# Moving two residual adds, a group of decay rates and one weight load around the start of a selective scan

## The chip, the cores and the metric

The kernel runs on one core of a Trainium2 chip. The metric is the device time of one launch, in microseconds (us); lower is better. The core has five engines that run their own instruction streams in order and meet through semaphores: PE (matmuls), DVE (vector), ACT (scalar functions), POOL (a second vector engine) and SP, which in this kernel only issues transfers.

## The reference, cut to what matters

Four sequences of 256 tokens with 512 features (1024 tokens, eight blocks of 128) go through two layers.

```python
xn = layernorm(x)
x = x + latent_attention(xn) + W_down(silu(W_gate xn) * (W_up xn))   # layer 0
xn = layernorm(x)
x = x + mamba(xn) + (base + top-2 LoRA experts)(xn)                  # layer 1
```

The Mamba part of layer 1 sets the second half of the kernel. For each of 1024 inner channels d and 16 states n:

```python
xc = silu(causal_conv4(xn @ in_proj_x))           # [channel, token]
dt_r, B, C = rmsnorm of the three parts of xc @ x_proj
dt = softplus(dt_r @ dt_proj + dt_bias)
h[t] = exp(dt[t] * A) * h[t-1] + dt[t] * B[t] * xc[t]     # A = -exp(A_log)
y[t] = sum_n h[t] * C[t];  out = ((y + D * xc) * silu(z)) @ out_proj
```

## The kernel before

**Layer 0.** The program works through two halves of 512 tokens. Gate, up and attention of a half are interleaved; then `down` (L432) makes the feed-forward and attention output of one block of 128 tokens. It is a generator: two matmuls with the attention result, then 14 chunks of two matmuls (high and low half of the hidden values), then one DVE addition of the PSUM result `po` to `x` (L446). With the yields there are 16 steps for each block of the second half: 1, 14 and the addition. `ff` is the stream of these steps for blocks 4 to 7, and `go(ff, n)` takes the next n. The steps fill PE while layer 1 begins, sequence 0 first, which needs only blocks 0 and 1.

**Opening of layer 1 (L1004 to L1094).** For sequence 0: four pairs of channel chunks are projected (`px_mm`), convolved (`conv_in`, `conv_taps`) and put through SiLU. `aneg` = -exp(A_log) is made by four ACT instructions from `al`, which sixteen small transfers bring in (L596); they stand ahead of the convolution of the last pair (L1023). Then the projection `pp`, its norm, and the step sizes: `step_in` makes two chunks of dt (one PSUM tile, two matmuls, then Abs and Relu of each chunk), `step_exp` the four ACT instructions of the softplus. Chunk 0 of dt and dt*x is spread over the partitions by matmuls (`pdts`, `pdus`), all later chunks through DRAM (`send`, `spread`). `decays(0)` and `decays(1)` make the decay factors of the first two units.

**The loop (L1222).** A unit u is one group of four states of one chunk of 128 channels: 4 units to a chunk, 8 chunks to a sequence, 128 units in all. Each unit has four decay instructions on ACT (`decays`, emitted up to two units ahead), a product `bx` and a scan `h` on DVE (`scan_in` L863, `scan` L871), a product with C on POOL (`hc`, L885), and four matmuls that sum the states into `ysum` (`states_sum`, one unit later). Two units after a chunk's last one, `close_chunk` multiplies its `ysum` by the gate silu(z). Everything else hangs on a table by unit: `put` places a call ahead of the unit's scan, `put_late` behind it. In the first three units the loop also takes `ff` steps at the head of a unit: 12, 12, and the rest. So the addition of block 6 comes in unit 1 and that of block 7 in unit 2, both ahead of that unit's `bx` and scan.

**Buffers and queues that the change touches.** PSUM pool `psmm` has three tiles, used in turn by nearly all matmul results (`po`, `pdt`, `pz`, ...). SBUF tag `w_in` has three tiles for projection weights of 512 KB; in the first units they are also lent out (`lent`, L840): to the decays of units 1 and 3, the scan results of units 0 and 2, and hc of unit 0. Unit 1's scan result is lent the buffer of `u`, a tile of the step computation, and its `hc` that of `lw`. `open_act`, called in unit 2, gives layer 0's memory to a new pool `act` and has SP issue four layer-1 weights into it: `rl`, `bw`, `lb`, `ow` (272, 1024, 256 and 2048 KB). Two further decay tiles, used from unit 4 on, are in this pool too; so their first writes wait until PE has read layer 0's data for the last time. `load_z` issues the gate's weights of a pair of chunks, `pz_mm` multiplies by them, `gate_silu` makes the gate (with a table load on each side). SP's order in units 2 to 4 is: dt and dt*x of the second pair out to DRAM, gate weights of pair 0, the spread of dt of chunk 2, the four layer-1 weights, gate weights of pair 1.

Of the kernel before, what the change touches and what calls it, by code (L numbers as in the profile page):

```python
# [11 lines left out]
AF = mybir.ActivationFunctionType  # L12
ALU = mybir.AluOpType
# [15 lines left out]
NG = 4  # L29
# [12 lines left out]
def block_kernel(  # L42
# [389 lines left out]
    def down(th, i):  # L432

        tb = 4 * th + i
        po = psmm.tile([P, D], F32, tag="mm", name="po")
        for hf in range(2):
            mm(po, lhsT=o8ns[th][:, hf, i * P : (i + 1) * P], rhs=m_att[:, hf, :],
               start=(hf == 0), stop=False)
        yield
        for m in range(MC):  # L440
            for j in range(2):
                mm(po, lhsT=hids[th][j][:, m, i * P : (i + 1) * P], rhs=wd[:, m, :],  # L442
                   start=False, stop=(m == MC - 1 and j == 1))
            if m < MC - 1 or th:
                yield
        nc.vector.tensor_tensor(x[:, tb, :], x[:, tb, :], po, ALU.add)  # L446
        yield

    def go(gen, n=1000):
        for _ in range(n):  # L450
# [311 lines left out]
        nc.scalar.copy(crows[b][:, 2 * i : 2 * i + 2, :], pc)  # L762


    def step_in(b, h, q):
        if q == 0:
            dts[b, h] = odd(h).tile([P, HALF, S], F32, tag="dt", name="dt")
            live["u"] = w1.tile([P, HALF, S], F32, tag="u", name="u")
        pd = psmm.tile([P, 2, S], F32, tag="mm", name="pdt")
        for i in range(2):  # L770
            c = h * HALF + 2 * q + i
            mm(pd[:, i, :], lhsT=dtw[:, c * P : (c + 1) * P], rhs=nrms[b][0:RK, :],
               start=True, stop=True)
        for i in range(2):
            j = 2 * q + i
            db = vec[:, h * HALF + j, V_DB : V_DB + 1]
            nc.scalar.activation(live["u"][:, j, :], pd[:, i, :], AF.Abs, bias=db)
            nc.scalar.activation(dts[b, h][:, j, :], pd[:, i, :], AF.Relu, bias=db)
# [232 lines left out]
    for p in range(NP):  # L1011
# [5 lines left out]
        if p < 3:  # L1017
            conv_in(0, p)
            conv_taps(0, p)
            go(ff, 1)  # L1020
    for n in range(NG):
        w = slice(n * NB, (n + 1) * NB)
        nc.scalar.activation(  # L1023
            aneg[w], al[w].rearrange("p k c (g n) -> p c k g n", n=NG)[:, :, :, :, n], AF.Exp
        )
    nc.gpsimd.tensor_scalar(aneg, aneg, -1.0, 1.0, ALU.mult, ALU.mult)

    px = live["px", 0, 3]
    nc.scalar.copy(pads[1][:, :, KC - 1 :], px)
# [4 lines left out]
    for i in range(2):  # L1034
# [11 lines left out]
        sel[:, 0 : NG * P].rearrange("p (k n j) -> p k n j", k=NG, n=NG),  # L1046
        ident.rearrange("p (k j) -> p k j", k=NG).unsqueeze(2).to_broadcast([P, NG, NG, NB]),
    )
    go(ff, 8)
    pp_mm(0, 0)  # L1050
    pp_mm(0, 1)
    pp_square(0)
    pp_norm(0)
    go(ff, 4)

    step_in(0, 0, 0)
    for j in range(2):
        step_exp(0, 0, slice(j, j + 1))
    b_rows(0, 0)
    c_rows(0, 0)  # L1060
# [3 lines left out]
    for j, eng in ((0, nc.vector), (1, nc.gpsimd)):  # L1064
# [1 line left out]
        eng.tensor_tensor(e[:, j, :], e[:, j, :], lw[:, j, :], ALU.add)  # L1066
        eng.tensor_tensor(dt[:, j, :], dt[:, j, :], e[:, j, :], ALU.add)
        eng.tensor_tensor(du[:, j, :], dt[:, j, :], xcs[0][:, j, :], ALU.mult)
    go(ff, 8)

    pdts = psx.tile([P, NG, S], F32, tag="bx", name="pdts")
    for k in range(NG):
# [16 lines left out]
    spread("du", 0, 1)  # L1089
    b_rows(0, 1)  # L1090
    c_rows(0, 1)
    step_in(0, 0, 1)
    step_exp(0, 0, slice(2, 4))
    decays(1)  # L1094

    def open_act():
        nonlocal act
# [19 lines left out]
    for b in range(B):  # L1117
        nxt = b + 1
        if b:
            put(b, 0, b_rows, b, 1)  # L1120
            put(b, 0, spread, "du", b, 1)

            for c in range(DC):
                put(b, c // 2, out_mm, b - 1, 1, c)
            put(b, 3, out_x, b - 1, 1)
            put(b, 4, dense, b - 1, 0, 0)
            put(b, 5, dense, b - 1, 0, 1)
            put(b, 5, expert_out, b - 1, 0)
            for c in range(DC):
                put(b, 6 + c, out_mm, b - 1, 0, c)  # L1130
            put(b, 15, out_x, b - 1, 0)
        else:
            for k in range(3):
                put(b, k, step_out, b, 0, 1, k)
            put(b, 2, step_x, b, 1)
            put(b, 2, load_z, b, 0)
            put(b, 4, load_z, b, 1)
            for p, u in ((0, 2), (1, 6)):
                for i in range(2):
                    put(b, u, pz_mm, b, p, i)  # L1140
            put(b, 4, gate_silu, b, 0)
            put(b, 8, gate_silu, b, 1)
        if b:
            put(b, 0, gate_silu, b, 0, 1)

# [76 lines left out]
    total = B * PER  # L1222
    late = []
    for u in range(total + 2):
        if u < 3:
            go(ff, 12 if u < 2 else 100)
        if 3 <= u < total - 2:
            decays(u + 2)
        for f, a in at.get(u, ()):
            f(*a)  # L1230
        if u < total:
            if u:
                scan_in(u)
        last = u - 2
        if last >= 0 and last % NU == NU - 1:
            c = last % PER // NU
            close_chunk(last // PER, c)
            if last // PER == B - 1:
                late.append(c)
        if u < total:  # L1240
            scan(u, 1 if u < total - 1 else 4)
            if u == 2:
                open_act()
            if u < 3:
                decays(u + 2)
        for f, a in late_at.get(u, ()):
            f(*a)
        if late and u >= total - PER + 22:
            c = late.pop(0)
            for i in range(2):  # L1250
                out_mm(B - 1, i, c)
        if 1 <= u <= total:
            states_sum(u - 1)
# [105 lines left out]
```

## Time and profile before

| quantity | value |
|---|---|
| median of 3 runs | 905.43 us (904.97 to 905.67) |
| the profiled execution's own time | 906.83 us |
| its span, first to last instruction | 905.0 us |
| busy, share of the span: PE, DVE, ACT, POOL | 84%, 76%, 58%, 54% |
| unit 0's scan begins | 363.23 us |
| the scans of units 1, 2, 3, 4, 5 begin | 374.47, 385.35, 389.01, 392.70, 398.57 us |
| mean of a scan, of a `bx`, of an `hc`, of a decay | 2234, 1231, 2308, 499 ns |

Times within the profile count from the span's start. The profiled execution lies 1.83 us around its span and 1.40 us over the median; a change is read as a difference of spans. In the profile's lines the parts are the start, the duration, the engine, the source line and operation, output and input, the count, and in brackets how long the engine was idle ahead of it and what ended that. SPq is SP's queue of transfers.

### The profile page before, as it was taken

The page shows a single profiled execution, that of the slowest core. Times are in us where ns is not written, and L with a number is a line of the kernel's source. Part 1 is how long each engine was busy: PE and PEld are TensorE (multiplying, and loading weights), DVE is VectorE, ACT ScalarE, POOL GpSimd, SP SyncE. Part 2 cuts the span into 40 slices and gives each one's busy share as a digit, 9 for nine tenths or more (in the row PEclk, how much of TensorE's full clock was granted, in tenths as well). Part 3 has the DMA queues.
Part 4 walks back from the last instruction along what each step waited for, and adds up shares of the span by engine and source line. Part 5 has one row for each costly group of instructions (what it writes and reads, how often), then busy time and mean ns, then how long its engine had stood idle before and what let it go on. Part 6 is the DMA issues. An engine that isn't in the chain of part 4 may idle for free.

```text
span 905.0 us, 10447 instructions
## 1 busy us (share of the span) xinstructions
PE 755.9 (84%) x3554; PEld 433.7 (48%) x3554; DVE 686.4 (76%) x675; ACT 525.5 (58%) x1005; POOL 489.4 (54%) x374
## 2 busy tenths in 40 slices
PE   5999989999989998876885898787898777976875
PEld 3665545666556576653542434443444443422421
DVE  4685553476573424486998999999999999999996
ACT  4234455213527356468768497778687785765661
POOL 4232222002223341456965969868789749797664
PEclk9999999999999999978786999987999888898997
DMA  6232232001222240394513453632635322436310
GB/s 209 67 85 80 83 93 70 12 0 35 59 58 70 59 114 26 78 306 116 151 47 93 124 144 100 168 94 61 172 116 176 82 79 85 117 89 170 88 28 23
DMA packets 67343, 86.67 MB, mean 96 GB/s; under 512 B 12077, under 2 KB 52025, under 8 KB 66906
## 3 DMA queue, kind: packets, MB, share of 16 engines
q1 hardware_dynamic: 57930, 67.12, 26.2%
q0 software_dynamic: 9072, 18.35, 7.3%
q8 instruction: 28, 0.46, 0.2%
q10 hardware_dynamic: 288, 0.52, 0.2%
q14 instruction: 25, 0.20, 0.1%
HBM read 66.58 MB, written 10.22 MB: 85 GB/s over the span
## 4 chain that ended last, share of the span: by engine, by line
PE 40%; DVE 32%; ACT 13%; POOL 6%; issue 5%; DMA 2%; SPq 1%; DVEq 0%; ACTq 0%; POOLq 0%
DVE h L881 19%; DVE bx L866 6%; ACT decay L860 5%; PE po L442 5%; PE pu L417 4%; PE pg L417 4%; PE sc L329 4%; POOL hc L885 3%; PE av L371 3%; PE scT L361 3%; PE pz L829 2%; PE pp L733 2%; PE ysum L897 2%; PE po L989 1%; ACT pe L363 1%
## 5 line engine op out<-in xcount | busy, mean ns | idle before, releaser
L885 POOL TENSOR_TENSOR hc<-h,cr 128x1024 f32<-128x1024 f32 (+1 forms) x131 | 302.0, 2308 | 121.0 <-DVE h L881 106.8
L881 DVE TENSOR_TENSOR_SCAN h<-decay,bx 128x1024 f32<-128x1024 f32 (+1 forms) x129 | 288.0, 2234 | 11.7
L860 ACT ACTIVATE decay<-dts,aneg 128x255 f32<-128x255 f32 x504 | 213.9, 499 | 117.8 <-DVE h L881 114.8
L897 PE MATMUL ysum<-hc,stack 128*32 128x256 f32 x1024 | 92.2, 431 | 89.5 <-POOL hc L885 89.2
L866 DVE TENSOR_TENSOR bx<-brow,dus 128x1024 f32<-128x1024 f32 x128 | 157.6, 1231 | 3.7
L429 POOL TENSOR_TENSOR hlo<-g,hhi 128x512 fp32r<-128x512 f32 x28 | 36.1, 1290 | 150.0 <-ACT hhi L428 150.0
L331 DVE TENSOR_REDUCE mpl<-sc 128x4 f32<-128x1024 f32 x64 | 77.3, 1223 | 23.7 <-PE sc L329 23.4
L897 PEld LDWEIGHTS ysum<-hc,stack 128*32 128x32 f32 x1024 | 21.9, 113 | 149.0 <-POOL hc L885 129.2
L400 POOL DMA_DIRECT2D wgu<-in_wgu x56 | 31.2, 557 | 90.8 <-PE pg L417 80.1
L363 ACT ACTIVATE pe<-scT 128x1024 f32<-128x1024 f32 x64 | 62.8, 1023 | 30.1 <-PE scT L361 29.8
L829 PE MATMUL pz<-xn1T,w_in 128*128 128x256 f32 x256 | 72.3, 433 | 6.8 <-DMA w_in<-in_inz 6.8
L989 PE MATMUL po<-ow,xc 128*128 128x512 f32 x128 | 72.3, 675 | 2.7 <-DVE xc L901 2.7
L689 PE MATMUL px<-xn1T,w_in 128*128 128x256 f32 x256 | 64.6, 400 | 2.3 <-ACT xn1T L681 1.6
L829 PEld LDWEIGHTS pz<-xn1T,w_in 128*128 128x128 f32 x256 | 52.1, 213 | 28.4 <-issue 12.2
L689 PEld LDWEIGHTS px<-xn1T,w_in 128*128 128x128 f32 x256 | 50.7, 202 | 22.4 <-issue 11.2
L425 DVE SCALAR_TENSOR_TENSOR g<-g,pg 128x512 f32<-128x512 f32 x28 | 19.2, 685 | 52.0 <-ACT g L424 52.0
L428 ACT CAST hhi<-g 128x512 fp32r<-128x512 f32 x28 | 17.4, 620 | 63.1 <-DVE g L427 62.7
L417 PE MATMUL pg<-xhi,wgu 128*128 128x512 f32 x112 | 46.6, 416 | 7.0 <-issue 4.5
L417 PE MATMUL pu<-xhi,wgu 128*128 128x512 f32 x112 | 47.7, 426 | 2.2 <-DMA wgu<-in_wgu 0.9
L442 PE MATMUL po<-wd,hhi 128*128 128x512 f32 x112 | 48.6, 434 | 0.0
L329 PE MATMUL sc<-km,qg 128*128 128x512 f32 x128 | 43.9, 424 | 3.3 <-ACT pe L363 2.8
L417 PE MATMUL pg<-xlo,wgu 128*128 128x512 f32 x112 | 44.8, 400 | 0.0
(213 smaller groups left out, 1249.4 us busy)
## 6 DMA issues: line engine op xcount, KB each, us to landing
dts<-dtd SPq DMA_DIRECT2D x124, 128.0 KB, 2.9
dus<-dud SPq DMA_DIRECT2D x124, 128.0 KB, 3.0
wgu<-in_wgu POOLq DMA_DIRECT2D x56, 256.0 KB, 2.8
w_in<-in_inz SPq DMA_DIRECT2D x16, 512.0 KB, 4.4
w_in<-in_inx SPq DMA_DIRECT2D x15, 512.0 KB, 4.4
dtd<-dt SPq DMA_DIRECT2D x15, 256.0 KB, 2.2
dud<-du SPq DMA_DIRECT2D x15, 256.0 KB, 2.2
wd<-in_wd POOLq DMA_DIRECT2D x7, 512.0 KB, 3.6
```

The source lines that it names most:

```text
L329: mm(sc[:, hp, :], lhsT=qs[b][:, gq, hf, qb * P : (qb + 1) * P], rhs=kms[b][:, 2 * hp : 2 * hp + 2, :], start=True, stop=True)
L331: nc.vector.tensor_reduce(mpl2[b % 2][:, qb, :, 16 + 2 * gq + hf].rearrange("p (a i) -> p a i", a=2), sc.rearrange("p a (i k) -> p a i k", ...
L417: mm(ps, lhsT=wgus[i][:, hc, :], rhs=xs[j][:, hc, :], start=(hc == 0 and j == 0), stop=(hc == HC - 1 and j == 1))
L442: mm(po, lhsT=hids[th][j][:, m, i * P : (i + 1) * P], rhs=wd[:, m, :], start=False, stop=(m == MC - 1 and j == 1))
L689: mm(px[:, i, :], lhsT=w[:, i, hc, :], rhs=xns[b][:, hc, :], start=(hc == 0), stop=(hc == HC - 1))
L829: mm(pz[:, i, :], lhsT=w[:, i, hc, :], rhs=xns[b][:, hc, :], start=(hc == 0), stop=(hc == HC - 1))
L860: nc.scalar.activation(da[:, k, 1:], live["dts", b, c][:, k, 1:], AF.Exp, scale=aneg[:, c, k, g : g + 1])
L866: nc.vector.tensor_tensor(bx, brow[g // 2][:, g % 2, :].unsqueeze(1).to_broadcast([P, NG, S]), live["dus", b, c], ALU.mult)
L881: nc.vector.tensor_tensor_scan(h[:, n].rearrange("p n t -> p (n t)"), da[:, n].rearrange("p n t -> p (n t)"), bx[:, n].rearrange("p n t -> ...
L885: nc.gpsimd.tensor_tensor(hc[:, n], h[:, n], crows[b][:, g, :].unsqueeze(1).to_broadcast([P, NG // parts, S]), ALU.mult,)
L897: mm(ysum[k * NB : (k + 1) * NB, :], lhsT=stack, rhs=hc[:, k, :], start=False, stop=(g == NU - 1))
L989: mm(live["po", b, i], lhsT=xcs[b][:, c, i * P : (i + 1) * P], rhs=late_w["ow"][:, c, :], start=False, stop=(c == DC - 1))
```

## The change

1. **The last two additions.** `down` no longer adds blocks 6 and 7; it leaves `po` in `live`, and `add_last` adds it behind the scan of unit 2 (block 6) and of unit 3 (block 7). The remaining `ff` steps of unit 2 are taken by a table entry behind the matmuls of the gate's pair 0, instead of at the head of the unit.
2. **A chunk's steps as a whole.** In the opening, `step_in` of the first pair is split by chunk: matmul, Abs, Relu and softplus of chunk 0, then those of chunk 1, each with a PSUM tile of its own. One `ff` step moves from ahead of these matmuls to behind them (4 and 8 become 3 and 9).
3. **The decay rates.** The four exponentials for `aneg` and its negation move from ahead of the last pair's convolution to behind the SiLU and the reload of the exponential tables.
4. **Decays of unit 1** move ahead of the steps of the second pair.
5. **The gate's weights.** `load_z` of pair 0 is issued in unit 1, not unit 2.

```diff
-        nc.vector.tensor_tensor(x[:, tb, :], x[:, tb, :], po, ALU.add)
+        if tb < 6:
+            nc.vector.tensor_tensor(x[:, tb, :], x[:, tb, :], po, ALU.add)
+        else:
+            live["last", tb] = po
         yield
+    def add_last(tb):
+        nc.vector.tensor_tensor(x[:, tb, :], x[:, tb, :], live.pop(("last", tb)), ALU.add)
...
-    def step_in(b, h, q):
-        if q == 0:
+    def step_in(b, h, q, part=(0, 1)):
+        if q == 0 and part[0] == 0:
...
-        for i in range(2):
+        for i in part:
             c = h * HALF + 2 * q + i
             mm(pd[:, i, :], lhsT=dtw[:, c * P : (c + 1) * P], rhs=nrms[b][0:RK, :],
                start=True, stop=True)
-        for i in range(2):
+        for i in part:
...
-    for n in range(NG):
-        w = slice(n * NB, (n + 1) * NB)
-        nc.scalar.activation(
-            aneg[w], al[w].rearrange("p k c (g n) -> p c k g n", n=NG)[:, :, :, :, n], AF.Exp
-        )
-    nc.gpsimd.tensor_scalar(aneg, aneg, -1.0, 1.0, ALU.mult, ALU.mult)
...
+    for n in range(NG):
+        w = slice(n * NB, (n + 1) * NB)
+        nc.scalar.activation(
+            aneg[w], al[w].rearrange("p k c (g n) -> p c k g n", n=NG)[:, :, :, :, n], AF.Exp
+        )
+    nc.gpsimd.tensor_scalar(aneg, aneg, -1.0, 1.0, ALU.mult, ALU.mult)
     go(ff, 8)
     pp_mm(0, 0)
     pp_mm(0, 1)
     pp_square(0)
     pp_norm(0)
-    go(ff, 4)
-
-    step_in(0, 0, 0)
+    go(ff, 3)
+
     for j in range(2):
+        step_in(0, 0, 0, (j,))
         step_exp(0, 0, slice(j, j + 1))
...
-    go(ff, 8)
+    go(ff, 9)
...
     c_rows(0, 1)
+    decays(1)
     step_in(0, 0, 1)
     step_exp(0, 0, slice(2, 4))
-    decays(1)
...
             put(b, 2, step_x, b, 1)
-            put(b, 2, load_z, b, 0)
+            put(b, 1, load_z, b, 0)
             put(b, 4, load_z, b, 1)
             for p, u in ((0, 2), (1, 6)):
                 for i in range(2):
                     put(b, u, pz_mm, b, p, i)
+            put(b, 2, go, ff)
             put(b, 4, gate_silu, b, 0)
             put(b, 8, gate_silu, b, 1)
+            put_late(b, 2, add_last, 6)
+            put_late(b, 3, add_last, 7)
...
-        if u < 3:
-            go(ff, 12 if u < 2 else 100)
+        if u < 2:
+            go(ff, 12)
```

In the order of instructions that results, PE has the 16 gate matmul passes of pair 0 ahead of the last 14 of block 7 instead of behind them. The gate weights of pair 0 take the buffer of unit 0's scan result, where before they took that of unit 1's decays; unit 3's decays go the other way round, and the gate weights of pair 1 take the buffer of unit 2's scan result, where before they took the one that pair 0's had held.

## The prediction

> **What bounds the kernel now.** I read the chain of waits around the scan's start first, then the timeline there engine by engine, then clock and transfers by stretch. After about 425 us the chain consists mostly of DVE's scans and what feeds them, which the change leaves alone: a shift of that point should reach the end whole. So the question is how much earlier the chain arrives there.
>
> The waits between 340 and 400 us:
>
> ```profile
> DVE x L446 <- PE po L442: 12.0, 2, 6.9
> PE pz L829 <- DMA w_in<-in_inz: 6.8, 1, 6.8
> ```
>
> The two additions of blocks 6 and 7 hold DVE, and behind them two scans, for 12.0 us. The timeline of DVE:
>
> ```profile
> 363.23 2.29 DVE L881 TENSOR_TENSOR_SCAN h<-decay,bx 128x1024 f32<-128x1024 f32 x1
> 372.46 0.69 DVE L446 TENSOR_TENSOR x<-x,po 128x512 f32<-128x512 f32 x1 [6.94 <-PE po L442]
> ...
> 381.80 0.69 DVE L446 TENSOR_TENSOR x<-x,po 128x512 f32<-128x512 f32 x1 [5.04 <-PE po L442]
> ```
>
> PE is solidly busy until 381.77, then stands still for 6.76 us, because the gate's weights are issued behind POOL's step work:
>
> ```profile
> 381.37 0.39 PE L442 MATMUL po<-wd,hlo 128*128 128x512 f32 x1
> 388.52 5.85 PE L829 MATMUL pz<-xn1T,w_in 128*128 128x256 f32 x16 [6.76 <-DMA w_in<-in_inz]
> 394.29 1.07 PE L897 MATMUL ysum<-hc,stack 128*32 128x256 f32 x16
> 395.30 0.66 PE L673 MATMUL pt<-cst,xnt 128*128 128x128 f32 x4
> ```
>
> The second gate product (401.57, 4.46 us) comes after these; its step matmuls release ACT at 407.12, and from there ACT is busy without a gap until scan 10. This is the path to shorten. SP's queue:
>
> ```profile
> 382.43 0.41 SPq L576 DMA_DIRECT2D w_in<-in_inz  x1
> 382.94 1.81 SPq L820 DMA_DIRECT2D dts<-dtd  x4
> 384.88 0.36 SPq L1105 DMA_DIRECT2D rl<-in_rl  x1
> 385.28 0.43 SPq L1105 DMA_DIRECT2D bw<-in_base  x1
> 385.76 0.43 SPq L1105 DMA_DIRECT2D lb<-in_lb  x1
> 388.40 0.33 SPq L1105 DMA_DIRECT2D ow<-in_ow  x1
> 394.39 0.33 SPq L576 DMA_DIRECT2D w_in<-in_inz  x1
> ```
>
> By the view of landing times the first gate weights land after 5.9 us (388.3), the last dts at 390.9, rl after 6.2 (391.1), lb after 8.5 (394.3), ow after 10.8 (399.2), the second gate weights after 7.0: 401.39, just ahead of their use at 401.57. The transfers queue.
>
> Stretches (columns after the busy times: clock, transfer share, GB/s):
>
> ```profile
> 366.00:382.00 16.00, 15.76 (x71) 11.40 (x69) 4.32 (x4) 7.04 (x16) 9.84 (x7) 1.00 0.11 26
> 386.00:388.50 2.50, 0.00 (x0) 0.01 (x1) 2.50 (x3) 2.50 (x6) 0.78 (x1) 0.51 1.09 244
> 388.50:392.00 3.50, 3.48 (x8) 2.85 (x9) 3.36 (x3) 3.48 (x7) 1.66 (x3) 0.50 1.06 340
> ```
>
> The first gate product ran at half clock, after PE's pause; transfers were nearly idle before 382 and full after.
>
> **The skill.** "TensorE: Matmul & The Clock Gate", What's actually happening: a PE left idle drops to half rate, a busy one returns to full. The trace agrees: 1.00 while busy, 0.50 after the pause. "DMA: Bandwidth & Descriptors", Queues, rings and completion order: SP has one ring on each of 16 DMA engines, consumed in ring order. The landings above agree. "ScalarE: Activation LUTs", What ACT_TABLE_LOAD costs: about 1283 ns a load; here 1.28 us. No load is added or removed.
>
> **The change part by part.**
>
> *Decay rates: 1.3 us gained.* Now they end at 339.53 because sixteen transfers arrive late (339.01), and the last pair's copy starts at 339.56. Its matmuls end at 334.61+3.61=338.22 and ACT is free at 337.30, so it can start at 338.26: 1.3 earlier, with convolution, SiLU and `pp` behind it. PE's eight fill-in steps end at 342.71 and the SiLU would at 342.8, so PE's 1.81 us wait at `pp` shrinks to 0.5. The new place costs nothing: the table load ends at 345.1, three exponentials take 1.32 and one 0.42, so 346.8, while `pp` ends at 348.17-1.3=346.9. Without that cover it costs up to 1.74. The negation on POOL (0.30) lies in POOL's 17.2 us gap.
>
> *Steps by chunk, one fill-in step moved: 0.* ACT and DVE get dt of chunk 0 some 3 us earlier, but `pdts` waits for PE's queue: it started at 357.52 when the fill-in ended, while dt was there at 357.07. PE's work up to it is only reordered, so it comes at 356.2. An extra PSUM tile costs no wait: its former holder was read by the norm.
>
> *Decays of unit 1 first.* Four instructions, 1.70 us. The step chain behind them, 1.3 earlier, loses that again: POOL's L795 starts at about 367.5 (was 367.74). It releases `u`, the buffer of scan 1, so scan 1 starts at 368.9 instead of 374.47; hc 0 runs 368.8 to 371.2, hc 1 372.5 to 374.8. The decays were not what scan 1 missed.
>
> *Additions behind scans 2 and 3.* The 12.0 us stall goes, but not the 12.0 us. Scan 2 writes over hc 0 and must await unit 0's state sums, which stand behind block 7's first seven chunks: 378.36-1.3=377.1. So scan 2 starts at 377.1 (was 385.35); addition 6 (0.69) follows, scan 3 at 381.5.
>
> *Gate weights.* They take scan 0's buffer, free when hc 0 ends at 371.2; SP waits there, with nothing urgent behind (the next send is ready at 376.2). Transfers are idle, and the shortest landing of this size in the trace is 3.9 us: about 375.3. PE reaches the product at 377.0, at full clock; equal shapes took 3.6 to 3.7 us there (px at 322.51 and 330.70). So 377.0 to 380.7, then seven chunks of block 7, 3.48 us: **PE's last read of layer 0 at 384.2**, was 381.77. I call it T4. It is later, since 3.7 us of work now stand ahead and only 1.3 were gained. Unit 3's decays now wait for scan 1 (371.2) and are wanted at 381.5: free.
>
> At T4 the new pool opens. DVE's addition 7 (384.25), the decays of units 4 and 5, the tables and SP's four weights follow. Was: ACT 384.63, SP 384.88. So ACT gains only 0.4 here, but then no longer waits for the gate product (2.18 us) or anything else: 3.29 decays, 1.50 normalise, 1.69 decays, 1.28 load, 0.60 gate; from 384.2 with overlaps the gate is done at 392.5. Unit 0's chunk closes, scan 5 starts at 392.9 (was 398.57, gain 5.7). The sums of unit 4 end at 394.9, was 401.51: gain 6.6.
>
> But now the second gate weights. SP issues them at 386.0, their buffer being free since hc 2 (381.8), behind rl, bw, lb and ow. The first gate weights and the spread have left the queue; ow no longer waits for a semaphore of the former (it was issued at 388.40, right after that landing). With an empty queue, rl lands about 3.0 us after 384.25 (a 256 KB send took 2.2, a 128 KB spread 2.9 in median): 387.2. Then as before from rl's landing to that of the second gate weights: 401.39-391.1=10.3. So 397.5. The product starts at about 397.55 instead of 401.57: **gain 4.0**, and ACT's gapless stretch shifts by it (407.12 to 403.1; ACT itself is ready by 399.2). Later weights keep their distance: pair 0 of the next sequence would land by about 402 and is used at 405.
>
> Sum: 4.0 off the span, 905.0 to 901.0; off the median, 905.43 to 901.4. Its terms: the 16.5 us from rl's issue to that landing become 13.25, because two transfers have left the queue (3.25), and rl is issued 0.6 earlier. The span's own execution took 906.83; its 1.83 outside the span are left as they are, and the median is moved by the same 4.0.
>
> **Rivals.**
>
> 1. *Transfers do not bind.* If they land by 394.9, the sums of unit 4 decide and 6.6 are gained: 898.8. For it: ow alone moved at about 430 GB/s (2.1 MB in 4.9 us), and the queue's head is light. Against: 4.2 MB from 384.25 in 10.6 us means nearly 400 GB/s with the start included, above the 340 of 388.5 to 392.
> 2. *Half the gain is lost on the way.* The gate product at half clock (5.85) moves T4 by 2.1 and the weights with it: gain 1.9, 903.5. Or the rates' new place hides badly: gain 2.7. Against the first: PE pauses nowhere near 4 us before 384.
> 3. *Slower: the first gate weights late.* In PE's order they now stand ahead of block 7's rest; each us late moves T4, hence pool, decays and weights, one for one. It decides from T4 of 388.2, that is if PE gets them after 381.0, 5.7 late. 10.2 us landings exist (402.49), but in a full queue; this one starts in an empty one. If hc 0 or SP's order held the issue back to 377.1, we are there; issued at 380, they land at 384.1, T4 is 391.3, the second weights land at 404.6, and the time is 908.4.
> 4. *The full stall is gained*, 12.0+1.3: 892. Against: the three buffers and T4 above.
> 5. *Nothing arrives.* The later stage has its own waits (4.70 of DVE on ACT at 423, transfers at 449), and the queue may cost as long as before from the start of rl: gain 0.6, 904.8.
>
> **How the numbers follow.** A gain of 4.0 (900.2 to 902.8) has 0.54; rival 1 0.14; rival 2 0.14; rival 5 and its like, within 0.2% (1.81 us, about what a measurement of this kernel can tell from no change), 0.09; slower 0.07; rival 4 and other large gains 0.02. Faster: 0.54+0.14+0.14+0.02=0.84. The predicted time is the first case's, 901.4. The range 898.4 to 904.2 holds that case, nearly all of rivals 1 and 2 and a little of 5: about 0.82. It includes both bounds of the unknown clock (3.7 and 5.85) and of the second landing (394.9 or before, to 400.3).
>
> **What would show it.** The pad copy at about 338.3; scans 0, 1, 2 at about 361.9, 368.9, 377.1; the first gate product ahead of block 7's end in 3.7 us, with no wait on its weights; last po at 384; no wait of DVE on po over 1 us; the second gate product waiting on its weights, at about 397.5; ACT's first step instruction behind it at about 403; from 430 on everything about 4 us earlier. Wrong, if PE waits on the first gate weights, if T4 is past 386, or if the shift at 430 is not the shift at the end.

## The result and the profile after

| | kernel before | changed kernel |
|---|---|---|
| median of the executions timed together (20 each) | 905.98 us | 904.53 us |
| lowest to highest | 904.59 to 911.43 | 900.85 to 907.29 |
| ratio of the times, 95% interval | | 0.9972 (0.9958 to 0.9985) |
| the profiled execution: own time, span | 906.83, 905.0 us | 904.87, 903.1 us |

The change makes the kernel 0.28% faster, of about 906 us some 2.5 us (1.4 to 3.8). The forecast was 4.0 us of gain, from 905.43 to 901.4, with a range up to 904.2. The kernel before was itself slower in these executions, 905.98; the measured ratio on the forecast's own 905.43 gives 902.9, and the median as it stands, 904.53, lies 0.3 us above the range. The sign holds; the gain is 1.5 us smaller than forecast, and 4.0 lies outside of the interval. The chain of waits holds up to scan 8; what fails is the term for the second gate weights.

Layer 0, which the change leaves alone, took longer in this profile. The pad copy of the third channel pair, the last ACT step that no part touches, starts at 335.25; before it was 334.35. So 0.90 us of what follows comes from ahead of the change. Below, "adjusted" means with this difference taken out, for each kernel by its own pad copy. Scan n is the scan of unit n; "half clock" is a granted clock of about 0.50 in a stretch; a transfer lands when its data has arrived.

The scans in the changed kernel, against the kernel before and against the forecast:

| scan | before | after | shift, adjusted | start, adjusted | forecast |
|---|---|---|---|---|---|
| 0 | 363.23 | 362.85 | -1.28 | 361.95 | 361.9 |
| 1 | 374.47 | 369.70 | -5.67 | 368.80 | 368.9 |
| 2 | 385.35 | 378.22 | -8.03 | 377.32 | 377.1 |
| 5 | 398.57 | 393.44 | -6.03 | 392.54 | 392.9 |
| 8 | 409.60 | 404.46 | -6.04 | | |
| 10 | 426.01 | 426.24 | -0.67 | | about -4 |
| 16 | 453.24 | 452.23 | -1.91 | | about -4 |
| 118 | 860.47 | 858.44 | -2.93 | | about -4 |

For the scans listed the forecast holds to 0.4 us up to scan 5, and up to scan 8 6.0 us are won. Between scans 8 and 10, 5.4 of them are lost. Then 2.3 us appear that the forecast doesn't know: 1.2 at scan 16, 0.4 at scan 21, and 0.6 at scans 87 and 97. The section on why the prediction was right or wrong comes back to them. DVE's timeline of the changed kernel shows the first half:

```profile
369.70 2.29 DVE L888 TENSOR_TENSOR_SCAN h<-d,bx 128x1024 f32<-128x1024 f32 x1 [3.30 <-POOL e L802]
...
378.22 2.29 DVE L888 TENSOR_TENSOR_SCAN h<-decay,bx 128x1024 f32<-128x1024 f32 x1 [3.51 <-PE ysum L904]
380.42 0.66 DVE L454 TENSOR_TENSOR x<-x,po 128x512 f32<-128x512 f32 x1
...
386.43 0.67 DVE L454 TENSOR_TENSOR x<-x,po 128x512 f32<-128x512 f32 x1
```

The 12.0 us wait of the additions on `po` is gone. Scan 1 now waits for POOL's last read of `u`, scan 2 for unit 0's sums: the two buffers that the prediction named. PE's timeline:

```profile
377.92 3.72 PE L836 MATMUL pz<-xn1T,w_in 128*128 128x256 f32 x16
384.75 1.07 PE L904 MATMUL ysum<-hc,stack 128*32 128x256 f32 x16
...
395.02 1.08 PE L904 MATMUL ysum<-hc,stack 128*32 128x256 f32 x8
400.48 5.78 PE L836 MATMUL pz<-xn1T,w_in 128*128 128x256 f32 x16 [4.38 <-DMA w_in<-in_inz]
406.18 1.13 PE L779 MATMUL pdt<-nrm,dtw 32*128 32x256 f32 x4
```

The first gate product stands ahead of block 7's end, without a wait, at full clock. The second could start when the sums of unit 4 end, at 396.1, but waits 4.38 us for its weights, and then takes 5.78 us where it took 4.46. So it ends at 406.26, adjusted 405.4, where it ended at 406.03: of the 6 us 0.7 are left. ACT waits for the step matmuls (`pdt`) behind it and from there works without a gap, and DVE's scan 10 comes at the end of that:

```profile
407.35 0.47 ACT L784 ACTIVATE u<-pdt,vec 128x256 f32<-128x256 f32 x1 [7.75 <-PE pdt L779]
...
426.24 2.29 DVE L888 TENSOR_TENSOR_SCAN h<-decay,bx 128x1024 f32<-128x1024 f32 x1
```

From the product's end to scan 10 it is 19.98 us here. In all twelve profiles in which this product stands in unit 6, of whatever kernel, it is 19.98 to 20.03 us, though scan 10 itself lies anywhere from 423.3 to 434.2. So in these runs scan 10 moves with the end of the second gate product and with nothing else, and two numbers decide: when its weights land, and how long it takes. SP's queue after PE's last read of layer 0:

```profile
384.85 0.36 SPq L1112 DMA_DIRECT2D rl<-in_rl  x1
385.25 0.43 SPq L1112 DMA_DIRECT2D bw<-in_base  x1
385.73 0.43 SPq L1112 DMA_DIRECT2D lb<-in_lb  x1
386.20 0.43 SPq L1112 DMA_DIRECT2D ow<-in_ow  x1
387.17 0.33 SPq L583 DMA_DIRECT2D w_in<-in_inz  x1
387.60 1.82 SPq L827 DMA_DIRECT2D dus<-dud  x4
390.35 0.35 SPq L583 DMA_DIRECT2D w_in<-in_inx  x1
```

The view of the transfers gives the time from issue to landing as the last number:

```profile
ow<-in_ow SPq DMA_DIRECT2D x1, 2048.0 KB, 11.4
...
w_in<-in_inz SPq DMA_DIRECT2D x1, 512.0 KB, 13.2
rl<-in_rl SPq DMA_DIRECT2D x1, 272.0 KB, 2.8
```

`rl` lands at 387.65, `ow` at 397.6, the gate weights at 400.37: 15.5 us after `rl`'s issue, where the forecast had 13.25. Between them the engines are nearly full all the time. The stretches (clock, transfer share, GB/s at the end):

```profile
392.00:394.00 2.00, 0.50 1.06 451
394.00:396.00 2.00, 0.50 0.93 348
396.00:398.00 2.00, 0.50 1.01 231
398.00:400.00 2.00, 0.50 1.08 203
```

At the end the share is about 1, but the rate falls to half of what it was, and PE's clock is at half. The chain of waits runs through the same place:

```profile
387.17 13.18 DMA w_in<-in_inz
400.34 0.14 issue
400.48 5.78 PE pz L836 x16
```

### The profile page after: what moved, and what is told of

It is laid out like the page before. It is cut to its first block, busy times and chain, and to the rows that moved or that the text cites. A ratio compares the mean times of both kernels' runs of the same rounds, so it can differ in the third digit from the quotient of the medians.

```text
span 903.1 us, 10448 instructions
## 1 busy us (share of the span) xinstructions
PE 749.8 (83%) x3554; PEld 432.4 (48%) x3554; DVE 687.3 (76%) x675; ACT 525.4 (58%) x1005; POOL 489.1 (54%) x374
## 4 chain that ended last, share of the span: by engine, by line
PE 38%; DVE 33%; ACT 15%; issue 4%; POOL 4%; DMA 4%; SPq 1%; DVEq 0%; ACTq 0%; POOLq 0%
DVE h L888 20%; ACT decay L867 7%; DVE bx L873 6%; PE po L442 5%; PE pu L417 5%; PE pg L417 4%; PE sc L329 4%; PE av L371 3%; PE scT L361 3%; PE pz L836 2%; POOL hc L892 2%; PE pp L740 2%; DMA w_in<-in_inz 1%; ACT pe L363 1%; PE ysum L904 1%
## 5 line engine op out<-in xcount | busy, mean ns | idle before, releaser
L904 PE MATMUL ysum<-hc,stack 128*32 128x256 f32 x1024 | 89.8, 420 | 94.9 <-POOL hc L892 94.5
L363 ACT ACTIVATE pe<-scT 128x1024 f32<-128x1024 f32 x64 | 62.8, 1023 | 29.8 <-PE scT L361 29.5
L836 PE MATMUL pz<-xn1T,w_in 128*128 128x256 f32 x256 | 69.7, 421 | 4.4 <-DMA w_in<-in_inz 4.4
```

The lines of the kernel that those rows point to most:

```text
L836: mm(pz[:, i, :], lhsT=w[:, i, hc, :], rhs=xns[b][:, hc, :], start=(hc == 0), stop=(hc == HC - 1))
L904: mm(ysum[k * NB : (k + 1) * NB, :], lhsT=stack, rhs=hc[:, k, :], start=False, stop=(g == NU - 1))
```

## The experiments

Two theories of the lost 5.4 us were open. **Queue:** the second gate weights stand behind 3600 KB of layer-1 weights, above all `ow` (2 MB, first used in unit 32), and PE's wait then costs half clock as well. **Elsewhere:** ACT's chain or the x weights of the next sequence bind at unit 9 anyway, so that the gate weights only seem to. Within the first a second question: does the place in the queue decide alone, or do transfers issued behind the weights hold them up too?

All in one table; the gain in us is the ratio's difference from 1 times 906. The runs were timed in three groups of 6 to 22 executions each, beside which the kernel before had medians of 907.26 (the two halves, `ow` late, gate weights first), 906.57 (nothing behind, before with `ow` late, both gates in unit 4) and 905.75 (gate weights late). So between groups only the ratios compare; a difference between two rows carries both intervals, some 2 to 3 us. "Landing" is from `rl`'s issue to the second gate weights, "product" the duration of the second gate product, scan 10 its adjusted shift against the first profile of the kernel before.

| kernel | median | ratio to before (95%) | gain | landing | product | scan 10 |
|---|---|---|---|---|---|---|
| kernel before, two profiles | 905.98 | 1 | | 16.5, 18.3 | 4.46, 6.31 | 0, +5.96 |
| changed kernel, two profiles | 904.53 | 0.9972 (0.9958-0.9985) | 2.5 | 15.5, 15.5 | 5.78, 5.48 | -0.67, -0.96 |
| opening alone | 905.46 | 0.9979 (0.9962-0.9995) | 1.9 | 18.1 | 3.69 | -0.51 |
| additions and gate alone | 905.98 | 0.9994 (0.9980-1.0008) | 0.5 | 15.2 | 5.71 | +0.65 |
| changed, `ow` late | 902.12 | 0.9935 (0.9910-0.9959) | 5.9 | 9.0 | 5.82 | -3.54 |
| changed, gate weights first | 902.44 | 0.9954 (0.9935-0.9973) | 4.2 | ahead of `rl` | 6.77 | -2.60 |
| changed, nothing behind | 900.04 | 0.9928 (0.9903-0.9953) | 6.5 | 14.2, 12.9 | 6.69, 6.74 | -1.06, -2.27 |
| before, `ow` late | 905.33 | 0.9980 (0.9966-0.9994) | 1.8 | 14.3 | 3.72 | -1.48 |
| changed, gate weights late | 912.37 | 1.0068 (1.0046-1.0090) | -6.2 | 15.0 | 5.89 | +8.73 |
| both gates in unit 4 | 898.61 | 0.9914 (0.9891-0.9937) | 7.8 | ahead of `rl` | 3.69 | -7.83 |
| both gates in unit 4, `ow` late | 896.31 | 0.9886 (0.9865-0.9908) | 10.3 | ahead of `rl` | 3.69 | -11.16 |

### The two halves of the change

Parts 2 to 4 alone on the kernel before, and parts 1 and 5 alone on it. The edits are those of the diff above; their core:

```diff
 # opening alone
+    go(ff, 3)
+    for j in range(2):
+        step_in(0, 0, 0, (j,))
...
+    decays(1)
     step_in(0, 0, 1)
 # additions and gate alone
+            put(b, 1, load_z, b, 0)
+            put(b, 2, go, ff)
+            put_late(b, 2, add_last, 6)
+            put_late(b, 3, add_last, 7)
```

> Parts 2, 3 and 4 alone on the kernel before (opening of layer 1); additions and gate weights as before. Theory (the prediction's first term: the pad copy 1.3 us earlier, carried by everything up to the second gate product, which in the kernel before waits for no transfer): last read of layer 0 by PE at about 380.5 instead of 381.8, second gate product at about 400.3 instead of 401.6, scan 10 1.3 us earlier, time 1.3 us below before (ratio 0.9986). Rival (the second gate weights, which landed only 0.2 us ahead of their use, bind as they do in the changed kernel): scan 10 at most 0.5 us earlier and a time within 0.5 us of before. Second rival (the whole measured gain of the change comes from the opening): 2.5 us below before.

> Parts 1 and 5 alone on the kernel before (additions behind the scans, gate weights of pair 0 a unit earlier); opening as before. Theory (the second gate product waits for its weights, and these land a fixed 15.6 us behind PE's last read of layer 0): last read at about 385.2, landing at about 400.8, PE idle some 4 us ahead of the product and so at half clock, 5.8 us instead of 4.46; the product ends near 406.6 (before: 406.0), scan 10 0 to 0.9 us later than before, although scan 5 is some 4 us earlier. Time between 1.5 us below and 0.6 us above before. Rival (the prediction's sum: 4.0 less the 1.3 of the opening): second gate product about 2.7 us earlier, time 2.7 us below before.

PE's timeline of the opening alone:

```profile
401.34 3.69 PE L829 MATMUL pz<-xn1T,w_in 128*128 128x256 f32 x16 [1.13 <-DMA w_in<-in_inz]
```

The 1.3 us are there: scans 0 to 4 are adjusted 1.3 us earlier. But now the second gate product waits 1.13 us for its weights, and by scan 10 only 0.5 is left. So in this stage the first rival was right. The time fell by 1.9 us all the same, against the rival's at most 0.5; the interval (0.5 to 3.4) holds the theory's 1.3 and the second rival's 2.5 as well and decides nothing. That the kernel before varies in this stage is seen in its second profile, below.

PE's timeline of additions and gate alone:

```profile
401.59 5.71 PE L836 MATMUL pz<-xn1T,w_in 128*128 128x256 f32 x16 [4.08 <-DMA w_in<-in_inz]
```

This is the theory's case: last read at 386.2, landing 15.2 us behind `rl`'s issue, half clock, the product's end at 407.3. Scan 5 is 4.4 us earlier (adjusted), scan 10 0.65 later, of which 0.3 come from a later arrival of `al` in this execution (ACT waits 0.88 us for it, before 0.59). The larger part of the diff yields nothing that could be told from zero (0.5, -0.7 to 1.8); all its early gain is lost at this one wait and the half clock behind it. The two halves add up to 2.4, against 2.5 of the whole, but each is known to 1.5 us only.

### What is ahead of the second gate weights

```diff
 # ow late: in open_act
-            nc.sync.dma_start(late_w[n], d)
+            if n != "ow":
+                nc.sync.dma_start(late_w[n], d)
...
+            put(b, 12, load_ow)
 # gate weights first: in the loop
-            put(b, 4, load_z, b, 1)
...
             if u == 2:
+                load_z(0, 1)
                 open_act()
```

> The changed kernel, with the transfer of ow (2 MB, first used in unit 32) issued in unit 12 instead of ahead of the second gate weights. Theory (the gain of 5.1 us that the scans of units 5 to 8 show is lost because the second gate weights stand behind ow): the weights land at about 391 to 394, ahead of the end of the sums of unit 4 (396.1); the second gate product starts at about 396.2 and waits for no transfer, ends at 400 to 402, ACT's first step instruction behind it at 401 to 403 instead of 407.35; scan 10 is 4.3 to 6 us earlier than in the changed kernel, and the time about 5 us below it, 899.5 (ratio to before 0.993). Rival (ACT or the weights of the projection x bind there anyway): scan 10 at most 1.5 us earlier and 903 to 905. Second rival (ow in unit 12 now collides with the weights of the gate's pair 3 or the step transfers): gain at scan 10, but lost again by unit 24.

> The changed kernel, with the second gate weights issued in unit 2 ahead of the four layer-1 weights, so that they await only hc 2, not PE's last read of layer 0. All other transfers keep their order. Theory (place in the queue): they land at about 387.5 instead of 400.4, the second gate product starts at about 396.2 and ends at 400 to 402; the x weights behind ow land as before, at about 401 to 402, and may hold the next projection by a little; scan 10 3.5 to 6 us earlier than in the changed kernel, time about 899.5 to 901.5 (ratio to before 0.993 to 0.996). Rival (the transfers as a whole bind, not their order: the same bytes must go before the x projection): the wait moves to the x weights and the gain over the changed kernel stays under 1.5 us.

PE's timeline with `ow` late:

```profile
397.88 5.82 PE L836 MATMUL pz<-xn1T,w_in 128*128 128x256 f32 x16 [1.47 <-ACT dt L785]
```

With the gate weights first:

```profile
397.38 6.77 PE L836 MATMUL pz<-xn1T,w_in 128*128 128x256 f32 x16 [1.47 <-ACT dt L785]
```

The weights land 9.0 us after `rl`'s issue in the first and before 387 in the second, and in neither does PE wait for them. Scan 10 comes 2.9 and 1.9 us earlier than in the changed kernel's first profile, where 4.3 to 6 and 3.5 to 6 were expected; of a gain over the changed kernel of about 5 and of 3 to 5 us, 3.4 and 1.7 came. The 3.4 are clear of noise (the intervals of the two ratios taken together leave 0.8 to 5.9), the 1.7 are not. So moving nothing but the one transfer `ow` wins time, and "Elsewhere" is refuted as the whole story. But a smaller rest of it is true. In both runs the product now waits for ACT's last reading of `pdt`, which frees its PSUM tile, until 397.8 and 397.3, 1.5 us past the sums; and it still runs at half clock. With `ow` late PE had paused for 3.10 us ahead of 389.2, and its clock was 0.50 from 392 to 402, though it was busy for 3.92 of the 4.00 us from 392 to 396. That is the part of my expectation that failed.

### What is behind them

```diff
-            put(b, 4 * c - 4 + o, spread, "du", b, c)
+            put(b, 7 if b == 0 and c == 2 else 4 * c - 4 + o, spread, "du", b, c)
...
-                put(b, 2 * p if b else (5, 6, 7, 8)[p], load_x, nxt, p)
+                put(b, 2 * p if b else (7, 7, 7, 8)[p], load_x, nxt, p)
```

> The changed kernel; the spread of dt*x of chunk 2 (four transfers of 128 KB) and the first x weights of the next sequence are put two to three units later in SP's program, behind the spread of dt of chunk 3, which in the changed kernel was issued at 396.1. So nothing stands right behind the second gate weights in SP's queue for some 8 us; what stands ahead of them (rl, bw, lb, ow) is untouched. Theory A (the transfers behind share the engines with the weights and hold up their landing): landing 8.5 to 10.5 us after issue instead of 13.2, at about 396 to 397.7; the product starts at about 397 to 398, ACT's first step instruction behind it at 402.5 to 404. Theory B (strict order of the queue, only what stands ahead counts): landing 12.5 to 13.5 us after issue as before, product at about 400.4. The time itself says little here, as dt*x of chunk 2 and the x weights now come later and may hold scan 8 and the next projection by 1 to 3 us: 901 to 905.

It was profiled a second time, and so was the changed kernel:

> Same kernel as the run with dt*x of chunk 2 and the first x weights behind in SP's queue, whose profiled execution (904.91) was the slowest of its six, the others at 897.5 to 901.9. Theory (the place and length of PE's half clock differ between executions): landing of the second gate weights again 11.5 to 12.5 us after issue, but a shorter second gate product, 3.7 to 5.8 us instead of 6.69, or a shorter first x projection; own time 898 to 902. Rival (the time lies outside of this stage): stage as in the first look to within 0.5 us.

> The changed kernel once more, for what is a matter of the execution and what of the kernel. Theory: second gate weights land 12.7 to 13.7 us after issue, PE idle ahead of the product for 4 to 5 us, product at half clock for 5.5 to 6.8 us, ACT's first step instruction behind it 22 to 23.5 us after PE's last read of layer 0 (22.5 in the first look); own time 901 to 907. Rival: landing or product differ by over 1.5 us, so that the first look can't stand for the kernel.

The landing in the first profile with nothing behind, by the view of the transfers:

```profile
w_in<-in_inz SPq DMA_DIRECT2D x1, 512.0 KB, 11.9
```

And in the second:

```profile
w_in<-in_inz SPq DMA_DIRECT2D x1, 512.0 KB, 10.6
```

In the changed kernel it is 13.2 in both profiles, which agree on everything else in this stage too (idle 4.38 and 4.37, product 5.78 and 5.48, scan 10 -0.67 and -0.96). Here the weights land 1.3 and 2.6 us sooner with the very same bytes ahead of them; nothing is issued behind them until the spread of dt of chunk 3, at 395.6 and 394.8, 3.0 and 1.7 us ahead of the landing. Two other runs have the changed kernel's queue at this place, additions and gate alone and gate weights late; they give 12.9 and 12.7. So with the transfers behind it is 12.7 to 13.2 in four profiles, without them 11.9 and 10.6 in two. Strict order (theory B, 12.5 to 13.5) falls; what the transfers behind take is 0.8 to 2.6 us by these profiles, no better known than that. Theory A's 8.5 to 10.5 was too low; what stands ahead is most of it. The Trainium skill, "DMA: Bandwidth & Descriptors", Queues, rings and completion order, says that descriptors are consumed in ring order, but that data descriptors carry no barrier, so that a later one may finish its write before an earlier one. In the prediction I had used only the first half of this. The page doesn't say that a later transfer delays an earlier one, and by which way it does so no run here shows.

The expectation of the second profile failed: the product was again at half clock (6.74), and the landing, 10.6, came below the 11.5 to 12.5 expected. So of the earlier landing only 0.4 and 1.6 us arrive at scan 10, against the changed kernel's first profile. And the time, 900.0, is lower than the 901 to 905 expected, and lower than these two profiles show: both executions (904.91 and 902.98) lie above the median. What the other executions gain is open.

### Is the change worth more once the queue is cleared?

The edit of `ow` late on the kernel before:

```diff
+            put(b, 12, load_ow)
```

> The kernel before, with ow issued in unit 12. Theory (without the change the second gate product is held by the sums of unit 4, which end at 401.5, so that the queue is worth nothing by itself): product at 401.3 to 401.6, scan 10 within 0.8 us of before, time 0 to 1 us below before; the change would then be worth about 5 us once ow is out of the way. Rival (ow itself slows the stage: the first gate product, the spreads, the x weights): scan 10 at least 2.5 us earlier and a time at least 2.5 us below before, so that most of the gain of the changed kernel with ow late isn't the change's.

```profile
401.07 3.72 PE L829 MATMUL pz<-xn1T,w_in 128*128 128x256 f32 x16
```

The product in PE's timeline waits for nothing and starts 0.7 us earlier (adjusted); running at full clock it takes 3.72 instead of 4.46 us, so scan 10 is 1.5 us earlier, more than the 0.8 expected and less than the rival's 2.5. The time fell by 1.8 (0.5 to 3.1), which doesn't shut out the rival's 2.5. With the early `ow` the change is worth 2.5 us; with the late one 5.9 less 1.8, about 4.1, which the two intervals together leave at 1.5 to 6.7. That the 4.1 meets the forecast's 4.0 is luck: there the transfer no longer binds at all, and ACT's hold on the PSUM tile and the half clock set the end.

### The slower rival, built

Part 5 undone in the changed kernel, so that the first gate weights are late while their product stands ahead of block 7's end.

```diff
-            put(b, 1, load_z, b, 0)
+            put(b, 2, load_z, b, 0)
```

> The changed kernel with part 5 undone: the gate weights of pair 0 are issued in unit 2 again, behind POOL's step work, while their product stands ahead of block 7's last seven chunks. This is the place of the prediction's slower rival. Theory (each us of their lateness moves PE's last read of layer 0 one for one, and the second gate weights and the rest with it): issued at about 379, landing 4 to 6 us later at 383 to 385, product at half clock until 388.5 to 391, last read at 392 to 395 instead of 384.8, second gate product 6 to 9 us later than in the changed kernel, time 4 to 8 us above it (907 to 911), slower than before. Rival (the later transfers have slack to give, since the first gate weights, the spread and the layer-1 weights then queue as one): last read as late, but the second gate product at most 3 us later, time within 2 us of before.

PE's and DVE's timeline:

```profile
383.61 6.31 PE L836 MATMUL pz<-xn1T,w_in 128*128 128x256 f32 x16 [7.03 <-DMA w_in<-in_inz]
...
393.19 0.69 DVE L454 TENSOR_TENSOR x<-x,po 128x512 f32<-128x512 f32 x1 [8.11 <-PE po L442]
...
408.36 5.89 PE L836 MATMUL pz<-xn1T,w_in 128*128 128x256 f32 x16 [3.92 <-DMA w_in<-in_inz]
```

PE's last read of layer 0 comes at 393.1 (adjusted 393.7; changed kernel 383.9), 9.7 us later, and nearly all of it passes on: scan 10 is 9.4 us later than in the changed kernel. The prediction's rival said slower from a last read of 388.2, one for one: 393.7 less 388.2 is 5.5, measured 6.2 (4.2 to 8.2). So part 5 is what makes part 1 bearable: without it the time is some 8.7 us worse than with it, somewhat over the 4 to 8 expected.

### A version that beats both

From these runs: put the second gate weights ahead, `ow` behind, and the second gate product into PE's idle time behind block 7, before its clock falls; then both gates need one pair of table loads.

```diff
-            for p, u in ((0, 2), (1, 6)):
+            for p, u in ((0, 2), (1, 4)):
...
-            put(b, 4, gate_silu, b, 0)
-            put(b, 8, gate_silu, b, 1)
+            put(b, 4, gate_silu, b, 0, 1)
```

> The changed kernel with ow in unit 12, the second gate weights ahead of the layer-1 weights, the second gate product in unit 4 instead of 6 (into PE's idle time behind block 7) and both gates made by one pair of table loads in unit 4, none in unit 8. Theory (from unit 5 on the end is set by ACT's chain, and its idle time before the step instructions of unit 6 is PE's delivery of the second gate product): the product starts at about 387.5 to 388.5, ends at 391.5 to 394; ACT goes on from 385 to the convolution of the next sequence without a gap of over 2 us; its step instructions of unit 6 at 399 to 401 (changed kernel: 407.35; with ow late: 404.79); scan 10 6 to 10 us earlier than with ow late (423.7), time 892 to 897. Rival (with the gate gone the x weights of the next sequence or POOL's taps bind): scan 10 at most 3 us earlier than with ow late, time 899 to 901.

> As the run with both gates in unit 4, but with ow where the changed kernel has it. It tells whether ow still costs anything once the second gate weights stand ahead of it. Theory (what ow delayed was the second gate weights alone): the second gate product as there, the x weights land at about 401 to 402 and hold the next projection (wanted at about 401) by at most 2 us; time 0 to 2 us above that run. Rival (ow and what stands behind it fill the engines until 404 and hold the dt*x of chunk 2 and the x weights by more): 3 to 5 us above that run.

PE's and ACT's timeline with `ow` late:

```profile
386.56 3.69 PE L836 MATMUL pz<-xn1T,w_in 128*128 128x256 f32 x16 [1.08 <-DMA w_in<-in_inz]
...
392.13 1.08 ACT L842 ACTIVATE sz<-pz 128x512 f32<-128x512 f32 x2
...
399.84 0.47 ACT L784 ACTIVATE u<-pdt,vec 128x256 f32<-128x256 f32 x1
...
401.93 3.78 PE L696 MATMUL px<-xn1T,w_in 128*128 128x256 f32 x8 [1.12 <-ACT xn1T L688]
```

And with `ow` in its old place, PE's:

```profile
406.21 3.75 PE L696 MATMUL px<-xn1T,w_in 128*128 128x256 f32 x8 [6.79 <-DMA w_in<-in_inx]
```

The product takes 3.69 us after a pause of only 1.08, ACT's step instructions come at 399.84 instead of 407.35, and the time falls by 10.3 us (8.3 to 12.2), within the expected 892 to 897. What the order of the weights, the place of the product and the saved table loads are each worth in this was not separated. With `ow` ahead of them the x weights become the late ones: PE waits 6.79 us for them where at most 2 were expected, and 2.3 us of the time are lost again, a little over the theory's 0 to 2.

### The kernel before, once more

> The kernel before once more. In its first profile scan 16 begins 6.22 us behind scan 15; in the profile of the changed kernel and of the others in which the gates stand where they were it is 4.93 to 5.02 us, which gives back 1.2 to 1.3 us of what was lost by unit 10, far from the change. Theory (that is a matter of the one execution: the x projection at 446.0 ran at half clock): scan 16 begins 4.9 to 5.1 us behind scan 15; scans 1, 2 and 5 begin 11.2, 22.1 and 35.3 us behind scan 0 as in the first profile, scan 10 62.8 us behind it to within 1.3 us. Rival (a matter of the kernel: the later stage of the kernel before meets its transfers worse): 5.9 to 6.5 us again.

This execution took 912.20. Its timelines of ACT and PE:

```profile
340.72 0.42 ACT L1023 ACTIVATE aneg<-al 32x128 f32<-32x128 f32 x1 [1.25 <-DMA al<-in_vec]
...
346.12 5.33 PE L733 MATMUL pp<-xc,xpw 128*64 128x256 f32 x16 [2.46 <-ACT xc L1040]
...
406.63 6.31 PE L829 MATMUL pz<-xn1T,w_in 128*128 128x256 f32 x16 [2.20 <-DMA w_in<-in_inz]
```

The late step at scan 16 is gone: it begins 4.99 us behind scan 15, so the 1.2 us that the first profile lost there were a matter of that execution, as the theory had it. Scans 1 and 2 keep their distances too. The rest of the expectation failed: scan 5 comes 34.5 us behind scan 0, not 35.3, and scan 10 66.4, not 62.8. Where the first profile of the same kernel had 0.59 us of wait on `al`, this one has 1.25; PE's pause ahead of `pp` grows from 1.81 to 2.46, `pp` runs at half clock (5.33 instead of 3.64), and scan 0 is 2.3 us later (adjusted). And the second gate weights, which landed 0.2 us ahead of their use in the first profile, come 2.20 us late, with 6.31 us of product behind them. They took 9.6 us from issue to landing, where they took 7.0 in the first profile; from `rl`'s issue it was 18.3 instead of 16.5. The adjusted scan 10 is 6.0 us later than in the first profile. An execution this slow is rare: of the 97 timed ones of the kernel before only two were slower.

## Why the prediction was right or wrong

- **Decay rates, 1.3 gained: right, in the execution that it was read from.** The pad copy came 5.21 us behind the third pair's before and 3.91 behind it after; 1.3, and nothing is paid in the new place (the rates end at 347.76, the next ACT step starts at 347.79). In all ten profiles with this opening scan 0 is 1.26 to 1.31 us earlier, adjusted. In the second profile of before the same wait cost 0.65 more and 1.7 of clock: a term that I took as fixed varies between executions.
- **Steps by chunk, decays of unit 1 first, 0 each: right as far as can be seen.** Scan 0 moved by the rates' 1.3 alone. Without the opening's parts scan 1 waits 3.25 us for ACT's decays instead of 3.30 for POOL, and comes 1.6 us later: the rates' 1.3 and the 0.3 of `al`. No run took these two parts alone, so that two small effects that cancel aren't shut out.
- **Additions: right.** The stall is gone, scans 1 and 2 are bound by the two buffers. Scan 3 came 1.8 us later than its 381.5, since its `bx` and the norm's `sh` stand on DVE between; nothing hung on it.
- **Gate weights of pair 0: right.** No wait, 3.72 us, last read at 383.9 against 384.2 (adjusted).
- **Landing of the second gate weights: wrong, and the step that failed.** "Then as before from `rl`'s landing to that of the second gate weights: 10.3" was 12.7 (387.65 to 400.37). With `rl` 0.4 us earlier than forecast, the landing came 2.0 us late. What I did not count was that SP, no longer held, also issues dt*x of chunk 2 and the first x weights 6 to 7 us earlier than before. In the kernel before these too were issued right behind the gate weights, but the gate weights themselves 6.0 us behind `ow` (388.40 and 394.39), when most of `ow`'s 10.8 us were over. In the changed kernel the gate weights follow `ow` after 1.0 us, and the other 1 MB follows them within 3.2 us, all while `ow` is moving. Keeping that 1 MB back gave 1.3 and 2.6 us of landing in the two profiles. I had asked what stands ahead in the queue, not what the change lets follow. And the 10.3 was read from one execution: the second profile of the kernel before has 11.8, and the opening alone, with the same queue, 10.7.
- **"The product at about 397.55", at its old length: a second term mis-sized.** It started at 399.6 (adjusted) and took 5.78, not 4.46. A pause of 2.6 us was in my own numbers (394.9 to 397.5), and it was 4.4; I asked for the clock only of the first product. The old length, 4.46, was again one execution's: the second profile of the kernel before has 6.31.
- **The sum.** The two terms given for the 4.0, 3.25 and 0.6, make 3.9; the last 0.1 is the product's start, 0.18 behind the landing before and taken as 0.05. 4.0 less 2.0 of landing less 1.3 of clock is 0.7 at scan 10, which is what that profile shows. This is the number of rival 5, "the queue may cost as long as before from the start of `rl`: gain 0.6", but not its cause: from the start of `rl` the queue cost 15.5 and not 16.5, and the clock took the rest.
- **The time** moved by 2.5 and not by 0.7, and why isn't shown. By the prediction's own sign, a shift at 430 that is not the shift at the end, it was wrong here: 0.7 at scan 10, 2.9 at scan 118. Of the difference, 1.2 at scan 16 and 0.4 at scan 21 are late steps of the first profile of the kernel before; its second profile loses neither the 1.2 nor 0.3 of the 0.4. The 0.6 at scans 87 and 97 are unexplained. On the other side that second profile loses 6.0 more by scan 10, where two profiles of the changed kernel lie within 0.3 us. How often either happens was not measured, so the part of the 2.5 that answers to each step can't be told, and that it came nearer to 4.0 than the 0.7 did is no support for the 4.0.
- **Rival 1** (transfers do not bind, 898.8, a gain of 6.6): with `ow` late 5.9, but for another reason at the end, ACT's hold on a PSUM tile and half clock. Its reading that `ow` alone moved at about 430 GB/s was misread: dt*x of chunk 2 and the x weights were issued at 394.83 and 396.72, before `ow` landed at 399.2. **Rival 2:** absent at the first gate product (3.72 us, full clock) and at the rates; the clock that it feared struck the second product. **Rival 3:** built as a run, it came at its price, 6.2 us for 5.5. **Rival 4:** absent.

## What to carry to other kernels

When a change frees a queue earlier, list what the queue will issue next, behind the transfer that you wait for, as well as what stands ahead of it: here both decided when it landed. Large weights with a distant first use are best put behind every transfer that is awaited soon; here 2 MB issued ten units later won 1.8 us in the kernel before and 3.4 in the changed one, whose own gain was 2.5. Price a wait of PE with the clock that follows it. And ask of each term read from one profile how near it stands to tipping: two terms of this forecast, 10.3 and 4.46, were 11.8 and 6.31 in a second profile of the very same kernel.

## What the runs showed of the hardware

- A transfer of 512 KB with the same bytes ahead of it landed after 12.7 to 13.2 us in four profiles with other transfers issued right behind it, and after 11.9 and 10.6 in two without.
- In the last 4 us before that landing the engines' share stayed at about 1 while the rate was 203 to 231 GB/s; at 392 to 394 it was 451.
- The same 16 matmuls of the gate took 3.69 us after a pause of 1.08 us, and 5.48 to 6.77 us where PE had paused for 1.5 to 4.4 us after a thin stretch. `pp` took 3.64 after pauses of 1.81 and 2.11 and 5.33 after 2.46. The pause just ahead doesn't decide alone: `pp` of the next sequence took 5.23 us in the changed kernel after a pause of 0.94. The Trainium skill, "TensorE: Matmul & The Clock Gate", What's actually happening, says that the clock goes by a window that runs freely and that the same kernel varies from run to run; the two executions of the kernel before fit this, 0.65 us of a late transfer having cost 1.7 us more.
- The second gate weights, issued at 382.7 ahead of the layer-1 weights, landed after 3.8 us; issued at 387.2 behind them, after 13.2: 4.5 us of earlier issue were worth 13.9.
